# Single source rows by byte addresses on two DMA queues, and a new order at the ends of two graph convolutions

## The chip, the core and the metric

The kernel runs on one core of one Trainium2 chip. The metric is the device time of one execution in microseconds (us), as the median of several runs: 6077.24 us before the change (three runs, 6076.54 to 6078.74). In the profile PE is TensorE (PEld its weight loads), DVE is VectorE, ACT is ScalarE, POOL is GpSimd, and SP is SyncE, which here only issues DMAs. "L767" is line 767 of the kernel before.

## The reference

A graph of N = 6250 nodes with 128 channels and E = 200000 edges, sorted by destination (the destinations are drawn as 6250·u², so low nodes have more edges); `src` is random. After a layer norm and a ReLU come two mesh convolutions and one attention, each over all edges:

```python
def mesh_conv(x, src, dst, ea, w1, b1, g, bt, w2, b2):
    m = jnp.concatenate([x[dst], x[src], ea], axis=-1) @ w1 + b1
    m = jax.nn.silu(group_norm(m, g, bt))
    m = m @ w2 + b2
    out = segment_sum(m, dst); cnt = segment_sum(ones, dst)
    return out / clip(cnt, 1)
h = mesh_conv(x, ...c1);  h = silu(group_norm(h, n1)) + (silu(t_emb) @ tm_w + tm_b)
h = mesh_conv(h, ...c2);  h = silu(group_norm(h, n2)) + x
q, k, v = h @ qw + qb, h @ kw + kb, h @ vw + vb          # 8 heads of 16
logits = (q[dst] * k[src]).sum(-1) * scale + (edge_attr @ ew + eb)
w = softmax of logits over the edges of each dst
o = group_norm(segment_sum(w * v[src], dst) @ ow + ob);  return x + h + o
```

## The kernel before

**Tiles and stages.** Edges lie in order of destination. A tile is 128 edges, a chunk eight tiles (1024 edges), so there are 196 chunks, the last with three tiles. The three stages (`conv(1)`, `conv(2)`, the attention) walk over the same chunks, and each has its own table in DRAM: `b_d` (x @ w1 of the source half, 512 bytes a node) for the convolutions, `kv_d` (keys and values, 1 KB a node) for the attention. The destination half is a product of one-hot matrices with the few table rows (`pk`) that a chunk's destinations span, since these lie close together.

**Fetching the source rows.** `gather` (L767) issues, for each tile, one indirect DMA on GpSimd's queue: 128 rows of the table, chosen by `src`. That is eight per chunk, put into one of the ring's buffers `g` (4 in the convolutions, 11 in the attention). A few chunks are "lone": their eighth tile is not gathered. Class `Rows` (L660) fetches it row by row over many steps: `list_of` loads the 128 node numbers of the tile as one row of a tile (L675), `step` (L678) reads ROWS = 12 of them into registers of SyncE (L689) and issues one DMA per row on SyncE's queue (L693) into the tile `row_g`, and `put` (L700) copies `row_g` into `g` on ScalarE. `by_rows` (L655) chooses the lone chunks: with 12 rows a step a chunk takes 11 steps, so the chunks 16, 27, ... 192, 17 in each stage.

**The steps.** `pipeline` (L878) emits, for each chunk n, one step of the program: `fetch` of chunk n + 2 (its `pk`, the comparison tiles `ohT` for two chunks at a time (L708, L711), and its gathers), then a step of `Rows`, products, roots, the second half of an earlier chunk, and so on; `put` of chunk n + 1 comes late in the step. Each engine runs its instructions in the order of the program (`in_order`). SyncE thus issues the row DMAs between the loads that feed TensorE.

**One chunk in a convolution.** TensorE makes the destination and attribute half (L1227), VectorE adds the gathered half (L1234), ScalarE squares, VectorE sums the squares per group (L1238), ScalarE takes the root (L1245), VectorE inverts and applies three operations (`normed`, L1248 to L1253), ScalarE the silu (L1254), TensorE sums into windows of 128 nodes (`summed`, L1259), ScalarE writes the sum twice under masks (`by_window`, L1264), VectorE adds to the table `U` in SBUF (L1269).

**Node batches.** When no later chunk can reach a window any more, the node part of the layer (`conv_nodes`, L1002: the second weight, group norm, silu, and the products that make the next stage's tables) runs on four windows at once, spread over the steps of the loop: it is a generator, and each step of the loop lets it go on to its next `yield`. `plan_batches` (L376) says at which step a batch starts: in the convolutions every eighth step from 81 to 185, 14 batches; each reads at run time which windows are done, and together they must reach 40 of the 49 windows. What they missed would be mended by a loop that reads its count at run time. `idle=4` makes a batch pause for six steps between its norm and its ends (four in the second convolution), but for the last one. The last nine windows are done after the loop by `last_nodes` (L1157).

**Attention.** `logits` (L1453 to L1459) multiplies the gathered keys with the queries, `maxima` (L1471) does the running maxima of several chunks at once, and per chunk follow the columns (`columns`, ScalarE, L1507, L1655, L1656), the weighted values (L1511), sums, a merge of maxima (L1551, L1525 to L1533) and a late addition. From chunk 170 on (BY_ACT) ScalarE makes the one-hot matrices as well (L1564).

Of the kernel before, what the change touches and what calls it, by code (L numbers as in the profile page):

```python
# [10 lines left out]
I32 = mybir.dt.int32  # L11
AF = mybir.ActivationFunctionType
# [9 lines left out]
P = 128  # L22
D = 128
# [8 lines left out]
BN = 4  # L32
LG = 2
# [4 lines left out]
ROWS = 12  # L38
# [13 lines left out]
def kernel(ctx: ExitStack, tc: tile.TileContext, x, src, dst, eat, w, out):  # L52
# [323 lines left out]
    def plan_batches(i):  # L376
# [278 lines left out]
    def by_rows():  # L655

        span, first = -(-P // ROWS), LG + 3
        return list(range(first + span, NCH - 1, span)), span

    class Rows:  # L660


        def __init__(self, pool, table_d, width):
            self.pool, self.table_d, self.width = pool, table_d, width
            self.chunks, self.span = by_rows()
# [3 lines left out]
            if self.chunks:  # L669
                self.list_of(self.chunks[0])  # L670

        def list_of(self, c):
            t = self.pool.tile([1, P], I32, name="row_at")
            col = c * TPC + TPC - 1
            nc.sync.dma_start(out=t, in_=src[:, col:col + 1].rearrange("p o -> o p"))  # L675
            self.at[c] = t

        def step(self, n):  # L678
            if n in self.starts:
# [6 lines left out]
            if self.now:  # L686
                c, e, t = self.now
                m = min(ROWS, P - e)
                _, at = nc.values_load_multi_w_load_instructions(  # L689
                    self.at[c][0:1, e:e + m], engines=[SP], min_val=0, max_val=N - 1,  # L690
                    skip_runtime_bounds_check_because="a source node")
                for j, a in enumerate(at):
                    nc.sync.dma_start(out=t[e + j:e + j + 1, :], in_=self.table_d[bass.ds(a, 1), :self.width])  # L693
# [184 lines left out]
    def pipeline(i, stage, aside=iter(())):  # L878
# [24 lines left out]
        for n, seconds in enumerate(todo):  # L903
            if n + ahead < NCH:
                ks[n + ahead] = stage.fetch(n + ahead)
            stage.rows.step(n)
# [21 lines left out]
            if n + 1 < NCH:  # L928
                stage.rows.put(ks[n + 1])
# [16 lines left out]
    class Nodes:  # L946
# [14 lines left out]
        def turned(self, t, m, tag="x", silu=None):  # L961
# [3 lines left out]
            if silu:  # L965
                nc.scalar.activation(out, tp, AF.Silu, bias=cols[f"{silu}_b"], scale=cols[f"{silu}_g"])
            else:
                nc.scalar.copy(out, tp)
# [33 lines left out]
    def conv_nodes(b, i, w, m, idle=0, last=False):  # L1002
# [26 lines left out]
        if i == 1 or last:  # L1029
# [5 lines left out]
            tT = b.turned(A, m, "t", silu=f"n{i}")  # L1035
# [21 lines left out]
        for rhs, bias, d_ in ends:  # L1057
            o = b.times(tT, m, rhs)
            if bias:
# [97 lines left out]
    def last_nodes(i, hx=True):  # L1157

        with tc.tile_pool(name="lastn", bufs=1) as lp, tc.tile_pool(name="lastp", bufs=6, space=PSUM) as ps:
# [621 lines left out]
```

## Time and profile before

| | |
|---|---|
| median of three runs | 6077.24 us |
| the profiled execution | 6073.33 us, its span on the core 6071.6 us |
| busy: TensorE | 3607.7 us (59%) |
| busy: VectorE | 4995.9 us (82%) |
| busy: ScalarE | 3351.4 us (55%) |
| busy: GpSimd | 4446.9 us (73%), 4638 gathers |
| mean granted TensorE clock | 0.754 |
| DMA | 760.21 MB, 125 GB/s |

A group of instructions is told with its line, engine, operation and tiles, its count, its busy time, the mean time of one, and behind the bar the idle time of the engine just before these instructions, with what ended that idle time ("issue" is time in which the engine waited for nothing that the profile shows). In a view in order of time each line has its start, its length, its engine and line, and in brackets the idle time before it and who ended it. "SPq" is SyncE's queue of instructions.

### The profile page before, as it was taken

To read this page: it belongs to the slowest core of one execution; us is meant where nothing else is said; L and a number is where in the kernel's file an instruction comes from. 1 tells how busy PE (TensorE), PEld (TensorE's weight loads), DVE (VectorE), ACT (ScalarE), POOL (GpSimd) and SP (SyncE) were. 2 spreads that over 40 slices of the span, in tenths; PEclk is the share of its full clock that TensorE was granted. 3 is DMA by queue.
4 is the path that set the end of the run, shared out by engine and by line. 5 is a ranking of instruction groups with operands and counts; after the bars stand their busy time and mean duration, and the time that the engine had idled before them with its cause. 6 is when DMAs were issued, how large, how long until landed. Compare 5 with 4: busy or idle time off the path is not lost. (4 is left out here: it accounts for less than half of the span.)

```text
span 6071.6 us, 88562 instructions
## 1 busy us (share of the span) xinstructions
PE 3607.7 (59%) x20941; PEld 3418.2 (56%) x20942; DVE 4995.9 (82%) x7118; ACT 3351.4 (55%) x5310; POOL 4446.9 (73%) x4687
## 2 busy tenths in 40 slices
PE   5565556556556555555666666655666665566665
PEld 4555555555556455555555655554555555565554
DVE  7888888888888588878888888865788888888888
ACT  5666666666666566666666666642333333333354
POOL 5777777777777477777777777757777777777775
PEclk8777777777777677777778777776777777777787
DMA  5454343444444343443444444435566666656663
GB/s 159 116 133 120 100 112 101 109 109 104 109 104 111 75 103 97 102 103 100 104 114 115 110 115 111 116 104 155 159 162 165 167 165 166 168 159 168 164 166 85
DMA packets 409874, 760.21 MB, mean 125 GB/s; under 512 B 102703, under 2 KB 276530, under 8 KB 379937
## 3 DMA queue, kind: packets, MB, share of 16 engines
q0 software_dynamic: 173152, 405.57, 26.4%
q1 hardware_dynamic: 230544, 345.24, 21.0%
q10 hardware_dynamic: 5632, 3.50, 0.2%
q8 instruction: 173, 2.83, 0.2%
q14 instruction: 373, 3.06, 0.2%
HBM read 707.36 MB, written 46.58 MB: 124 GB/s over the span
## 5 line engine op out<-in xcount | busy, mean ns | idle before, releaser
L767 POOL DMA_INDIRECT g<-b_d,src_i x3092 | 2931.6, 948 | 954.3 <-issue 904.4
L1259 PE MATMUL u<-h,oh 128*128 128x129 f32 (+1 forms) x6252 | 1265.1, 384 | 1388.4 <-ACT h L1254 1388.2
L1259 PEld LDWEIGHTS u<-h,oh 128*128 128x128 f32 x6252 | 1167.1, 288 | 1469.8 <-ACT h L1254 1465.4
L767 POOL DMA_INDIRECT g<-kv_d,src_i x1546 | 1470.0, 951 | 490.6 <-issue 439.8
L1227 PE MATMUL m<-pk,ohT 101*128 101x128 f32 x6252 | 961.7, 319 | 193.1 <-DVE h L1234 151.7
L1227 PEld LDWEIGHTS m<-pk,ohT 101*128 101x128 f32 x6252 | 932.7, 236 | 210.3 <-DVE h L1234 166.9
L1234 DVE TENSOR_TENSOR h<-m,g 128x1024 f32<-128x1024 f32 x392 | 475.8, 1214 | 477.4 <-DMA g<-b_d,src_i 462.8
L1518 PE MATMUL us<-v,oh 128*128 128x145 f32 x3126 | 590.3, 357 | 378.3 <-DVE flat L1543 329.3
L1518 PEld LDWEIGHTS us<-v,oh 128*128 128x128 f32 x3126 | 545.2, 248 | 418.1 <-DVE flat L1543 241.8
L1438 PE MATMUL qe<-pk,ohT 101*128 101x136 f32 x3126 | 558.1, 348 | 335.0 <-ACT ebs L1455 319.1
L1438 PEld LDWEIGHTS qe<-pk,ohT 101*128 101x128 f32 x3126 | 518.6, 249 | 367.6 <-ACT ebs L1455 360.8
L1254 ACT ACTIVATE h<-h 128x1024 f32<-128x1024 f32 x392 | 412.9, 1053 | 544.5 <-DVE h L1253 527.9
L1236 ACT ACTIVATE sq<-h 128x1024 f32<-128x1024 f32 x392 | 411.8, 1051 | 486.3 <-DVE h L1234 484.1
L733 ACT ACTIVATE ohT<-ohT,minus_p 96x1024 f32<-96x1024 f32 x588 | 669.3, 1138 | 19.6 <-DMA ohT<-rel_d 19.5
L734 ACT ACTIVATE ohT<-ohT 96x1024 f32<-96x1024 f32 x588 | 619.9, 1054 | 18.7
L1238 DVE TENSOR_REDUCE var<-sq 128x64 f32<-128x1024 f32 x392 | 475.0, 1212 | 105.8 <-ACT sq L1236 105.0
L1252 DVE TENSOR_TENSOR h<-h,cps 128x1024 f32<-128x1024 f32 x392 | 477.1, 1217 | 13.5
L1253 DVE TENSOR_TENSOR h<-h,cps 128x1024 f32<-128x1024 f32 x392 | 477.0, 1217 | 13.4
L790 DVE TENSOR_TENSOR oh<-cps,dm 128x1024 f32<-128x1024 f32 x392 | 474.1, 1209 | 2.1 <-PE u L1259 2.1
L1249 DVE TENSOR_TENSOR h<-h,cps 128x1024 f32<-128x1024 f32 x392 | 473.9, 1209 | 0.0
L1453 DVE TENSOR_TENSOR g<-qe,g 128x768 f32<-128x768 f32 (+1 forms) x391 | 251.2, 683 | 211.2 <-DMA g<-kv_d,src_i 203.9
L1531 ACT ACTIVATE us<-d 128x16 f32<-128x16 f32 x196 | 36.6, 187 | 638.2 <-DVE d L1527 566.3
(288 smaller groups left out, 4271.9 us busy)
## 6 DMA issues: line engine op xcount, KB each, us to landing
ohT<-rel_d SPq DMA_DIRECT2D x291, 768.0 KB
row_g<-b_d SPq DMA_DIRECT2D x4352, 0.5 KB
g<-b_d,src_i POOLq DMA_INDIRECT x3092
row_g<-kv_d SPq DMA_DIRECT2D x2176, 1.0 KB
pk<-a_d SPq DMA_DIRECT2D x588, 46.0 KB
g<-kv_d,src_i POOLq DMA_INDIRECT x1546, 3.1
ohT<-in_eat_dram SPq DMA_DIRECT2D x291, 40.0 KB
a_d<-n_o SPq DMA_DIRECT2D x28, 256.0 KB
```

The costliest lines, as they stand in the source:

```text
L733: nc.scalar.activation(k.ohT[:WN, :], k.ohT[:WN, :], AF.Square, bias=minus_p[:WN])
L734: nc.scalar.activation(k.ohT[:WN, :], k.ohT[:WN, :], AF.Relu, bias=1.0, scale=-4.0)
L767: h = nc.gpsimd.indirect_dma_start(out=g[:, t, :table_d.shape[1]], out_offset=None, in_=table_d, in_offset=bass.IndirectOffsetOnAxis(ap=k. ...
L790: return nc.vector.tensor_tensor(k.oh[:, :k.nt, :], iota[:, None, :].to_broadcast([P, k.nt, P]), k.dm[:, :, None].to_broadcast([P, k.nt, P ...
L1227: nc.tensor.matmul(k.m[:, t, :], lhsT=lhs[:, t * P:(t + 1) * P], rhs=rhs, start=(j == 0), stop=(j == len(terms) - 1))
L1234: nc.vector.tensor_tensor(k.mt, k.m[:, :n], k.g[:, :n], ALU.add)
L1238: return lambda: nc.vector.tensor_reduce(var[:, at:at + n * H], sq[:, :n].rearrange("p t (g c) -> p (t g) c", c=HD), AX.X, ALU.add)
L1252: nc.vector.tensor_tensor(k.mt, k.mt, over_edges(gam, k.nt), ALU.mult)
L1253: nc.vector.tensor_tensor(k.mt, k.mt, over_edges(bet, k.nt), ALU.add)
L1259: nc.tensor.matmul(k.u[:, 0, :wide], lhsT=k.oh[:, t, :], rhs=k.h[:, t, :wide], start=(t == 0), stop=(t == k.nt - 1))
L1438: nc.tensor.matmul(k.qe[:, t // TB, at:at + DB], lhsT=lhs[:, t * P:(t + 1) * P], rhs=rhs, start=(j == 0), stop=(j == len(terms) - 1))
L1518: nc.tensor.matmul(k.u[:, :wide], lhsT=k.oh[:, t, :], rhs=k.v[:, t, :wide], start=(t == 0), stop=(t == k.nt - 1))
```

## The change

It has five parts.

1. **Byte addresses and own semaphores.** The list of node numbers is multiplied on VectorE by the bytes of a row (`to_bytes`, four steps after the list was asked for), and the row DMA takes its source from a flat view of the table in bytes, at the register's value. All rows of a step but the last count on a semaphore of the `Rows` object (`landed`), not on those of the framework, and `put` waits for the full count.
2. **More rows.** ROWS goes from 12 to 16: a chunk takes 8 steps, and the lone chunks are 13, 21, ... 189, 23 in each stage. `put` moves to the start of the step.
3. **A second list in the attention.** Another `Rows` object issues nine rows a step on ScalarE's queue, at the end of the step behind the columns: a chunk takes 15 steps, and every 16th chunk from 25 to 185 is lone too, 11 more.
4. **Ends of the convolutions.** The batches start at steps 85 to 181 (13 of them). In the first convolution the last three go without idle steps, and the last two have a step between transpose and silu (`fine` 1), the last one also between each product and its copy (`fine` 2). Chunk 194 is normalised in two halves of four tiles, and before chunk 195 the window copies of 194 are not made first.
5. **The end of the second convolution.** A tile `below` of 12632 floats per partition that nobody uses puts the tiles of `last_nodes(2)` higher in SBUF.

```diff
-ROWS = 12
+ROWS = 16
+BY_SIDE = 9
+BELOW = 12632
...
-            if n % 8 == (4 if i == 3 else 1) and n > (40 if i == 3 else 80) and n + 6 < NCH \
+            if n % 8 == (4 if i == 3 else 5) and n > (40 if i == 3 else 80) and n + (6 if i == 3 else 10) < NCH \
...
-    def by_rows():
-        span, first = -(-P // ROWS), LG + 3
-        return list(range(first + span, NCH - 1, span)), span
+    def by_rows(m, every, first=LG + 3):
+        span = -(-P // m)
+        return list(range(first + span, NCH - 1, every)), span
...
+            self.bytes_d = table_d.rearrange("n c -> (n c)").bitcast(U8)
+            self.landed = [[tc.alloc_semaphore(f"{name}{j}"), 0] for j in range(2)]
...
+        def to_bytes(self, t):
+            nc.vector.tensor_scalar(t, t, 4 * self.width, None, ALU.mult)
         def step(self, n):
+            self.fresh -= 1
+            if self.fresh == 0:
+                self.to_bytes(self.at[max(self.at)])
...
                 for j, a in enumerate(at):
-                    nc.sync.dma_start(out=t[e + j:e + j + 1, :], in_=self.table_d[bass.ds(a, 1), :self.width])
+                    h = self.issue.dma_start(out=t[e + j:e + j + 1, :].bitcast(U8),
+                                             in_=self.bytes_d[bass.ds(a, 4 * self.width)][None, :])
+                    if j == m - 1:
+                        tc.declare_fence(h.ins, group=key)
+                        continue
+                    tc.no_tile_sem_insts.add(h.ins.name)
+                    h.then_inc(s[0], 16)
+                    s[1] += 16
...
         def put(self, k):
             if k.c in self.got:
-                nc.scalar.copy(k.g[:, TPC - 1, :self.width], self.got.pop(k.c))
+                s = self.landed[self.chunks.index(k.c) % 2]
+                nc.scalar.copy(k.g[:, TPC - 1, :self.width], self.got.pop(k.c)).wait_op(s[0], s[1], "sem-ge")
...
-            stage.rows.step(n)
+            if n + 1 < NCH and n + 1 in ks:
+                for r in stage.rows:
+                    r.put(ks[n + 1])
+            stage.rows[0].step(n)
...
             if n < NCH:
                 stage.early(ks, n, todo[n + 1])
-            if n + 1 < NCH:
-                stage.rows.put(ks[n + 1])
+            for r in stage.rows[1:]:
+                r.step(n)
...
-            tT = b.turned(A, m, "t", silu=f"n{i}")
+            tp = b.in_bank(A, m)
+            if fine > 0:
+                yield
+            tT = b.silu_of(tp, m, f"n{i}")
...
             o = b.times(tT, m, rhs)
-            if bias:
+            if bias or fine > 1:
                 yield
...
+            if i == 2:
+                es.enter_context(tc.tile_pool(name="below", bufs=1)).tile([P, BELOW], FP, name="below")
...
-            def normed(k):
+            def normed(k, by=TPC):
+                for a in range(0, k.nt, by):
+                    n = min(by, k.nt - a)
+                    mt = k.mt[:, a:a + n]
...
-                        if k.c >= NCH - SOON and self.sums:
+                        if NCH - SOON <= k.c < NCH - 1 and self.sums:
...
-                        normed(k)
+                        normed(k, TPC // 2 if k.c == NCH - 2 else TPC)
...
-                    for r in conv_nodes(nodes, i, w, BN, idle=4 if j + 1 < len(plans[i]) else 0):
+                    for r in conv_nodes(nodes, i, w, BN, idle=4 if j + (3 if i == 1 else 1) < len(plans[i]) else 0,
+                                        fine=(j + 3 - len(plans[i])) * (i == 1)):
...
-                self.rows = Rows(rw, kv_d, KV)
+                self.rows = [Rows(rw, kv_d, KV, "rows3"),
+                             Rows(side, kv_d, KV, "rows4", mybir.EngineType.Activation, BY_SIDE, 16, 10)]
```

More of the change, by code (lines that the diff above doesn't have):

```diff
@@ L653, with __init__ @@
         oh = pe = v = None
-    def by_rows():
-        span, first = -(-P // ROWS), LG + 3
-        return list(range(first + span, NCH - 1, span)), span
+    def by_rows(m, every, first=LG + 3):
+        span = -(-P // m)
+        return list(range(first + span, NCH - 1, every)), span
     class Rows:
-        def __init__(self, pool, table_d, width):
-            self.pool, self.table_d, self.width = pool, table_d, width
-            self.chunks, self.span = by_rows()
+        def __init__(self, pool, table_d, width, name, engine=SP, m=ROWS, every=-(-P // ROWS), first=LG + 3):
+            self.engine, self.m, self.issue = engine, m, nc.sync if engine == SP else nc.scalar
+            self.pool, self.table_d, self.width, self.name = pool, table_d, width, name
+            self.bytes_d = table_d.rearrange("n c -> (n c)").bitcast(U8)
+            self.chunks, self.span = by_rows(m, every, first)
+            self.landed = [[tc.alloc_semaphore(f"{name}{j}"), 0] for j in range(2)]
             self.starts = {c - 2 - self.span: c for c in self.chunks}
@@ L670, in __init__ @@
                 self.list_of(self.chunks[0])
+                self.to_bytes(self.at[self.chunks[0]])
+                self.fresh = 0
         def list_of(self, c):
-            t = self.pool.tile([1, P], I32, name="row_at")
+            t = self.pool.tile([1, P], I32, name="row_at", bufs=2)
             col = c * TPC + TPC - 1
@@ L687, in step @@
                 c, e, t = self.now
-                m = min(ROWS, P - e)
+                m = min(self.m, P - e)
                 _, at = nc.values_load_multi_w_load_instructions(
-                    self.at[c][0:1, e:e + m], engines=[SP], min_val=0, max_val=N - 1,
-                    skip_runtime_bounds_check_because="a source node")
+                    self.at[c][0:1, e:e + m], engines=[self.engine], min_val=0, max_val=(N - 1) * 4 * self.width,
+                    skip_runtime_bounds_check_because="where a source node's row begins")
+                s = self.landed[self.chunks.index(c) % 2]
+                key = f"{self.name}_{c}_{e}"
                 for j, a in enumerate(at):
-                    nc.sync.dma_start(out=t[e + j:e + j + 1, :], in_=self.table_d[bass.ds(a, 1), :self.width])
+                    h = self.issue.dma_start(out=t[e + j:e + j + 1, :].bitcast(U8),
[6 more added lines that the diff above has]
+                    s[1] += 16
+                    tc.add_to_no_dep_group(key, h.ins)
                 self.now[1] = e + m
@@ L959, in in_bank, with turned, silu_of @@
             return tp[:, :m, :]
-        def turned(self, t, m, tag="x", silu=None):
+        def turned(self, t, m, tag="x"):
             tp = self.in_bank(t, m)
             out = self.tile(m, tag)
[L965 to L968, printed above, removed]
+            nc.scalar.copy(out, tp)
+            return out
+        def silu_of(self, tp, m, n):
+            out = self.tile(m, "t")
+            nc.scalar.activation(out, tp, AF.Silu, bias=cols[f"{n}_b"], scale=cols[f"{n}_g"])
             return out
@@ L1000, in span, with conv_nodes @@
         return bass.ds(w, m) if not isinstance(w, int) else slice(w, w + m)
-    def conv_nodes(b, i, w, m, idle=0, last=False):
+    def conv_nodes(b, i, w, m, idle=0, last=False, fine=0):
         at = span(w, m)
@@ L1157, in last_nodes @@
     def last_nodes(i, hx=True):
[L1159 removed]
+        with ExitStack() as es:
+            if i == 2:
+                es.enter_context(tc.tile_pool(name="below", bufs=1)).tile([P, BELOW], FP, name="below")
+            lp = es.enter_context(tc.tile_pool(name="lastn", bufs=1))
+            ps = es.enter_context(tc.tile_pool(name="lastp", bufs=6, space=PSUM))
             n = NW - NWD
@@ L1278, in fetch @@
                     k.g = gp.tile([P, TPC, D], FP, name="g")
-                    gather(k, k.g, b_d[i], ring, self.rows.chunks)
+                    gather(k, k.g, b_d[i], ring, self.rows[0].chunks)
                     k.h = hs[c % len(hs)]
@@ L1356, in conv @@
             stage = Stage()
-            stage.rows = Rows(rw, b_d[i], D)
+            stage.rows = [Rows(rw, b_d[i], D, f"rows{i}")]
             nodes.var = lambda: stage.var[:, NV:]
@@ L1586, in fetch @@
                 k.g = gp.tile([P, TPC, KV], FP, name="g")
-                self.behind = gather(k, k.g, kv_d, ring, self.rows.chunks)
+                self.behind = gather(k, k.g, kv_d, ring, self.rows[0].chunks + self.rows[1].chunks)
                 return k
```

16 lines of the change are left out of this document (10 added, 6 removed).

## The prediction

> **What bounds it.** I read the page first, then GpSimd (POOL) in order of time, then the waits of SyncE's queue, then the two places between stages, then ScalarE in the attention.
>
> ```profile
> span 6071.6 us, 88562 instructions
> ...
> L767 POOL DMA_INDIRECT g<-b_d,src_i x3092 | 2931.6, 948 | 954.3 <-issue 904.4
> ...
> L767 POOL DMA_INDIRECT g<-kv_d,src_i x1546 | 1470.0, 951 | 490.6 <-issue 439.8
> ```
>
> GpSimd issues 4638 gathers of 0.95 us; nearly all its idle time before them is "issue", about 0.3 us each, so it waits for nobody. The table by stretches, cut where the rows of gathers begin and end (columns: length, then busy time and count of PE, PEld, DVE, ACT and POOL, granted clock, share of the DMA engines, GB/s):
>
> ```profile
> 56.00:1995.00 1939.00, 1144.99 (x6728) 1095.99 (x6726) 1609.67 (x1787) 1261.25 (x1555) 1467.04 (x1546) 0.75 0.44 112
> 2060.00:3995.00 1935.00, 1156.35 (x6747) 1104.44 (x6748) 1618.01 (x1660) 1251.04 (x1533) 1463.95 (x1546) 0.75 0.42 108
> 4049.00:5990.00 1941.00, 1184.46 (x6748) 1104.76 (x6748) 1593.07 (x3305) 739.94 (x2017) 1469.11 (x1546) 0.76 0.61 164
> 1995.00:2060.00 65.00, 34.40 (x172) 32.24 (x172) 35.90 (x66) 34.70 (x54) 5.95 (x3) 0.63 0.09 24
> 3995.00:4049.00 54.00, 29.75 (x176) 27.19 (x174) 32.59 (x60) 20.10 (x33) 6.04 (x2) 0.75 0.23 63
> 5991.00:6071.00 80.00, 33.65 (x191) 30.91 (x191) 63.76 (x151) 16.73 (x61) 24.84 (x35) 0.69 0.08 22
> ```
>
> Each stage is one unbroken row of 1546 gathers, so one costs 1939/1546 = 1.254 us, then 1.252 and 1.256. The three rows make 5815 us of the span. The rest is 56 us of preparation, two gaps of 65 and 54 us, and 80 us after the last gather. A change pays if it takes gathers out of the rows or shortens a gap.
>
> **The gathers.** Before, every 11th chunk from 16 to 192 has its eighth tile fetched by single rows: 17 chunks. After, SyncE does every 8th from 13 to 189, 23 chunks, and in the attention ScalarE's queue does every 16th from 25 to 185, 11 more, none of them twice. That takes 6, 6 and 17 gathers out: 7.5, 7.5 and 21.4 us. Near the end of the attention this stops paying, as the waits of VectorE there show, first for 4100 to 5600 us, then for 5730 to 6050 us:
>
> ```profile
> DVE g L1453 <- DMA g<-kv_d,src_i: 165.1, 49, 11.6
> ```
> ```profile
> DVE g L1453 <- DMA g<-kv_d,src_i: 7.9, 3, 5.1
> ```
> ```profile
> 5832.17 0.95 DVE L1453 TENSOR_TENSOR g<-qe,g 128x768 f32<-128x768 f32 x1
> ```
>
> VectorE lives on the gathers until chunk 178, whose first product this last row is, the last to start within 4 us of its gathers; then it has a backlog of its own. One gather of the 17 lies net behind chunk 178 (two by SyncE and one by ScalarE, where before there were two), so I count 16: 20.1 us. Sum: 35.1 us.
>
> **The price on SyncE.** It issues the rows between the loads that feed TensorE. Here are the instructions of a row (shortest/median/longest, ns), the load of a step's addresses, and one step of twelve rows:
>
> ```profile
> L693 SPq FUSED_REGOPS  x6528: 37/37/47, 95.0 to 5956.6; - x198
> ...
> L693 SPq DMA_DIRECT2D row_g<-b_d x4352: 224/228/1167, 95.1 to 3941.2; - x198
> ```
> ```profile
> L689 SPq TENSOR_LOAD <-row_at x561: 687/1007/2876, 93.9 to 5947.2; - x187
> ```
> ```profile
> 654.41 4.79 SPq L693 DMA_DIRECT2D row_g<-b_d  x12
> ```
>
> And SyncE's longest waits, from 400 to 1600 us in the first convolution and from 4400 to 5600 us in the attention (121 steps each; us in total, times, longest):
>
> ```profile
> SPq L708 <- PE m L1227: 130.0, 38, 7.1
> SPq L693 <- DMA ohT<-rel_d: 99.6, 61, 3.4
> ```
> ```profile
> SPq L693 <- DMA ohT<-rel_d: 136.3, 60, 5.4
> SPq L708 <- PE qe L1438: 136.0, 31, 9.5
> ```
>
> A row takes (4.79 − 0.23)/11 = 0.41 us when nothing holds it. With byte addresses the multiplication by the row's length should go: 0.037 us and about as much behind it, so 0.34 is my value, 0.41 the upper bound. Twelve rows and a load (1.01) were 5.95 us; sixteen are 6.6 us at 0.34, or 7.8 at 0.41, with 0.17 more for the load of sixteen addresses. So SyncE gets 0.65 to 1.8 us more per step. Its waits give 1.90 us a step in the convolution and 2.25 in the attention; the larger half of the landing waits goes too, since fifteen of sixteen rows now count on a semaphore of their own. It fits: no cost. If that cover is gone, SyncE is late with pk and ohT and everything stands behind it (the slower rival).
>
> [...]
>
> New on VectorE is one multiplication of a 1x128 list per lone chunk, 80 in all. The nearest row is a small one:
>
> ```profile
> 2040.21 0.17 DVE L1008 TENSOR_SCALAR n_c<-flat 128x3 f32<-128x3 f32 x1 [2.33 <-DMA wcl<-wc_d]
> ```
>
> 14 us, spread over stretches in which VectorE waits for gathers: nothing, and 0.2 us after chunk 178. It comes four steps after its list is asked for and four before SyncE reads it, so neither waits. The copy into place now stands at the head of ScalarE's step and waits for the rows; behind it are the root and the comparisons. The last rows are issued two steps, some 20 us, earlier: nothing.
>
> **The price on ScalarE.** Nine rows come after each step's columns. Here is ScalarE in the attention, from the end of the columns to what comes next:
>
> ```profile
> 5259.06 0.20 ACT L1656 CAST v<-ef 128x8 f32<-128x8 bf16 x1
> 5263.10 0.19 ACT L1531 ACTIVATE us<-d 128x16 f32<-128x16 f32 x1 [3.83 <-DVE d L1527]
> 5263.22 0.20 ACT L1533 ACTIVATE be<-d 128x16 f32<-128x16 f32 x1
> 5264.62 0.27 ACT L1455 COPY ebs<-qe 128x48 f32<-128x48 f32 x2 [1.20 <-DVE g L1453]
> ```
>
> The hole is 3.8 us, and 1.2 more before the next operation that VectorE asks for soon. Nine rows at 0.34 to 0.41 and a load of about 0.9 are 4.0 to 4.6 us: hidden within 5.0. In steps 179 to 182 ScalarE also makes the one-hot matrices (from chunk 170 on), and VectorE has no slack left there; I put 3 us on that; the bounds are 0 and 8 (2 us late in each of the four, see the rival). [...]
>
> **The first convolution's end.** The last gather ends at 1995 us, and the last chunk's use of it comes 26 us later; in the second convolution (3995 us) it is 7.6 us:
>
> ```profile
> 2021.11 0.55 DVE L1234 TENSOR_TENSOR h<-m,g 128x384 f32<-128x384 f32 x1
> ```
> ```profile
> 2005.95 0.58 ACT L1067 COPY n_o<-nd 128x512 f32<-128x512 f32 x1 [5.18 <-PE nd L974]
> ```
> ```profile
> 4002.60 0.55 DVE L1234 TENSOR_TENSOR h<-m,g 128x384 f32<-128x384 f32 x1
> ```
>
> ScalarE stands 5.18 us before the copy of a node batch, whose product was given to TensorE just ahead of it, while the next silu waits behind. The change starts the last batch at step 181 instead of 185, lets the last three go without idle steps, and puts a step between product and copy (and between transpose and silu). Its steps end at 193. I take a lag of 10 us in place of 26, nearer to the second convolution's, since one wait of this kind a step is what sets the two apart: 16 us; the bounds are 0 and 18.4. There are 13 batches instead of 14. They still reach the 40 windows: the last one counts on chunk 177, whose first edge goes to node 5127 in the list that the reference draws, and window 40 begins at 5120.
>
> **The end of both convolutions.** Chunk 194 is normalised in halves, and chunk 195 no longer stands behind the window copies of 194:
>
> ```profile
> 2028.85 1.06 ACT L1254 ACTIVATE h<-h 128x1024 f32<-128x1024 f32 x1 [2.82 <-DVE h L1253]
> 2033.80 0.72 ACT L1264 ACTIVATE u<-u,mask 128x129 f32<-128x129 f32 x2 [3.90 <-PE u L1259]
> ...
> 2036.70 0.72 ACT L1264 ACTIVATE u<-u,mask 128x129 f32<-128x129 f32 x2 [1.75 <-PE u L1259]
> ```
> ```profile
> 4018.34 0.68 DVE L1065 TENSOR_TENSOR n_o<-nd,r_qb 128x512 f32<-128x512 f32 x1
> ```
> ```profile
> 4036.95 4.94 SPq L1062 DMA_DIRECT2D kv_d<-n_o  x6
> ...
> 4044.01 1.80 SPq L1074 DMA_DIRECT2D h_d<-n_x  x3
> ```
> ```profile
> 4049.09 0.95 POOL L767 DMA_INDIRECT g<-kv_d,src_i  x1 [18.81 <-DMA ohT<-in_eat_dram]
> ```
>
> TensorE sums eight tiles in the 3.9 us from 2029.9 to 2033.8. With halves the first silu waits for three operations on half the width, some 0.65 us each by the 0.55 of the 384 wide row above, not for three at double that; it can start 1.9 us earlier and takes half as long, so TensorE begins near 2027.5 and ends near 2031.5; chunk 195's three tiles follow at once, to 2033.0 instead of 2036.7. I take 3.6 us, and 3.4 in the second convolution, whose order is the same; the bounds are 0 and 4. In the second convolution the last batch's query end (4018.34 to 4019.02) stands behind the loop, and SyncE still has to issue its write before the branch. Started four steps earlier, it ends at step 194: I take 2.0 us for the two and their signal, between 0.7 and 2.0, and 1.5 less lag. Last, the node tiles of the end lie 50 KB higher, above the attention's gather buffers. So the first gather no longer waits for the h_d writes (issued until 4045.81, first gather 3.3 us later), only for the kv_d writes (issued until 4041.89): 3.9 us, bounds 0 and 3.9.
>
> **Sum.** 35.1 + 16 + 3.6 + 3.4 + 2.0 + 1.5 + 3.9 − 3 = 62.5 us. The profiled execution took 6073.33 us (span 6071.6), 3.9 under the median of the three runs, so it stands for them: 6077.2 − 62.5 = 6014.7, given as 6015.
>
> **Rivals.** *The gathers alone* (chance 0.20): the lag at 1995 us comes from other things than the copies, and the first attention gather waits for something else in those buffers. Then 19.9 us go: 6035. For it speaks that VectorE's own work there is dense; against it, the 5.18 us wait.
>
> *SyncE sets the pace, slower* (0.06): at 0.41 us a row its spare 1.90 us is used up. From 0.417 on, each step is longer than the gathers'. At 0.43 (a row that waits a little) it is 0.21 us × 184 steps × 3 stages, 116 us, with the gathers' gain gone and some 27 us kept at the ends: 6165. For it: SyncE waits in most steps for an earlier landing. Against it: most rows leave that chain.
>
> *ScalarE late in the attention* (0.06): a row costs 0.54 us, as on SyncE with waits, so load and rows take 5.8 us in a hole of 3.8 to 5.0 and ScalarE is 0.8 to 2.0 us late. VectorE's spare is 165.1 us over 151 steps, 1.1 us each; from there on it decides. At 2.0 us, 0.9 us are lost in each of 165 steps, 149 us, the gathers' 20 with them: 6184. At the lower end little is lost: near 6035.
>
> *The transfers bind* (0.03): the share of the DMA engines in the attention is 0.61 (table above), and the same bytes move. Were that the limit, the attention's 20.1 us would stay: 6035. The gathers' 0.3 us "issue" before each speaks against it. [...]
>
> **How the numbers follow.** The forecast has 0.63, a rest of 0.02 is open. The range goes from 5998 (lag as in the second convolution or less, ScalarE at no cost, shorter steps) to 6045 (the gathers alone, with 8 us on ScalarE). Faster by over 0.2% (12 us, about what a measurement of this kernel can tell): forecast, gathers alone, transfers, half of ScalarE's case and the rest, 0.88; within 0.2%: 0.04; slower: 0.08.
>
> **What would show it.** After: 1540, 1540 and 1529 gathers at 1.25 us with "issue" before them; a row of SyncE near 0.34 us and no multiplication; the first gap near 45 us, the second near 43; ScalarE's nd waits (L1067) small after 1980 us; VectorE's waits for gathers in the attention still over 100 us. The forecast is wrong if gathers show waits for ring buffers, if SyncE's waits on TensorE vanish, or if the first gap stays near 65 us.

## The result, and the profile after

The changed kernel takes 6031.62 us (median of four runs, 6023.66 to 6035.83), the kernel before 6077.99 (four runs, 6076.54 to 6081.23): a ratio of 0.992, with a 95% interval of 0.990 to 0.994, or 46 us less. The forecast was 6015, 62.5 us less; 16 us of the sum are missing. The profiled execution of the changed kernel took 6035.83 us, the slowest of its four, with a span of 6033.9, against 6073.33 (3 us under the fastest of the four) and 6071.6 before. What follows compares these two executions first; their spans lie 38 us apart, not 46, so 25 us of the sum are missing between them.

The page of the changed kernel, span and gathers:

```profile
span 6033.9 us, 89776 instructions
...
L793 POOL DMA_INDIRECT g<-b_d,src_i x3080 | 2925.2, 950 | 953.8 <-issue 903.8
...
L793 POOL DMA_INDIRECT g<-kv_d,src_i x1529 | 1457.3, 953 | 482.7 <-issue 433.9
```

The counts are the forecast ones, 1540 a convolution and 1529 in the attention, and nearly all idle time ahead of them is still "issue": GpSimd waits for nobody. The table by stretches, cut as before where the rows of gathers begin and end (length, then PE, PEld, DVE, ACT, POOL busy, clock, DMA share, GB/s):

```profile
56.00:1991.00 1935.00, 1139.06 (x6758) 1090.93 (x6756) 1622.79 (x1811) 1276.68 (x1576) 1463.06 (x1540) 0.75 0.44 112
2034.70:3966.00 1931.30, 1143.54 (x6734) 1091.77 (x6734) 1617.94 (x1672) 1251.45 (x1537) 1462.05 (x1540) 0.74 0.42 108
4011.00:5937.00 1926.00, 1210.60 (x6654) 1132.06 (x6655) 1585.01 (x3304) 725.57 (x1989) 1457.28 (x1529) 0.75 0.62 165
1991.00:2034.70 43.70, 23.07 (x110) 21.58 (x110) 23.64 (x56) 20.24 (x34) 5.74 (x3) 0.66 0.09 25
3966.00:4011.00 45.00, 25.47 (x146) 23.52 (x146) 28.71 (x56) 18.75 (x32) 5.76 (x1) 0.73 0.15 42
5937.00:6034.00 97.00, 48.25 (x287) 44.35 (x286) 79.14 (x189) 34.58 (x108) 24.83 (x35) 0.76 0.09 25
```

Held against the table of before, the three rows of gathers are 4, 4 and 15 us shorter (the forecast had 7.5, 7.5 and 21.4), the gaps 21 and 9 us (forecast 19.6 and 10.8), and the tail after the last gather is 17 us longer: 97 us in place of 80 (16 us when both are taken from the end of the last gather, 97.0 and 80.7). So two things are off: the rows give about 13 us too little, and the tail takes 17 us where the forecast had some 4 (3 us for ScalarE's list and 1.3 us for the gather behind chunk 178).

**SyncE** did what the forecast said. One step of sixteen rows, and the two instructions of a row (shortest/median/longest, ns):

```profile
663.62 5.14 SPq L710 DMA_DIRECT2D row_g<-b_d  x16
```
```profile
L710 SPq MOVE row_g<-b_d x5888: 29/29/38, 95.6 to 3881.3; - x197
L710 SPq DMA_DIRECT2D row_g<-b_d x5888: 224/228/1266, 95.7 to 3881.3; - x197
```

The multiplication is gone, and a row takes (5.14 − 0.23)/15 = 0.33 us, where 0.34 was put.

**The first convolution's end.** The last chunk's addition, and VectorE's first node operation after the loop:

```profile
1996.02 0.55 DVE L1272 TENSOR_TENSOR h<-m,g 128x384 f32<-128x384 f32 x1
...
2013.89 0.17 DVE L1039 TENSOR_SCALAR n_c<-flat 128x3 f32<-128x3 f32 x1 [4.82 <-issue]
```

The addition comes 5 us after the last gather's end, not 26: 21 us gained, more than the 18.4 that the forecast set as the bound. ScalarE's waits for node products, 11.7 us from 1960 us on before, are gone from the same stretch. Behind it the halves save what they were to save: from the addition to the first node operation it takes 17.9 us, where it took 19.1, although VectorE stands 4.82 us ahead of that operation, where it stood 2.33 before; without these 2.5 us it is 3.7 us less, and the forecast had 3.6. "Issue" says that the profile has no releaser for the wait. The trace shows where it lies: VectorE's branch at the loop's end begins at 2009.46, its next instruction only at 2012.51, 3.0 us later, where before these two lie 0.6 us apart (2038.27 and 2038.83). Why, it does not show.

**The attention.** VectorE's longest waits from 4062 to 5560 us, then from 5690 to 6010:

```profile
DVE g L1496 <- DMA g<-kv_d,src_i: 108.4, 41, 10.1
DVE v L1554 <- ACT v L1550: 60.1, 34, 6.2
```
```profile
DVE flat L1580 <- ACT us L1574: 24.6, 5, 8.3
DVE lg L1502 <- ACT ebs L1498: 7.2, 3, 4.6
DVE v L1554 <- ACT v L1550: 6.5, 10, 2.2
```

The same waits before, from 4100 to 5600 and from 5730 to 6050 us:

```profile
DVE v L1511 <- ACT v L1507: 6.7, 18, 0.4
```
```profile
DVE flat L1537 <- ACT us L1531: 15.2, 4, 5.3
DVE v L1511 <- ACT v L1507: 3.2, 8, 0.5
DVE lg L1459 <- ACT ebs L1455: 2.0, 1, 2.0
```

In the first stretch nearly all of the 60 us of waits for ScalarE's copies are new, and the waits for gathers fall by about as much, from 165 to 108: VectorE's spare pays. In the second, the wait for the factors us (L1574) rises from 15.2 to 24.6 us and its longest from 5.3 to 8.3; with the two other waits for ScalarE it is 17.9 us more. Here is the step in which it happens, on ScalarE and on VectorE:

```profile
5795.26 1.06 ACT L1608 ACTIVATE oh<-oh 128x1024 f32<-128x1024 f32 x1
5797.55 3.05 ACTq L710 DMA_DIRECT2D row_g<-kv_d  x9
5800.64 0.19 ACT L1574 ACTIVATE us<-d 128x16 f32<-128x16 f32 x1 [4.33 <-issue]
```
```profile
5800.86 0.44 DVE L1580 TENSOR_TENSOR flat<-flat,us 128x272 f32 x1 [6.83 <-ACT us L1574]
...
5820.57 0.44 DVE L1580 TENSOR_TENSOR flat<-flat,us 128x272 f32 x1 [8.35 <-ACT us L1574]
```

The one-hot matrix ends at 5796.3; then come a load of addresses and nine rows, and only then the factors for which VectorE has been waiting since 5794.0. The chunks' first products, 2 to 13 us behind their gathers until chunk 178 in both executions, are 24.6 us behind at chunk 182 (11.3 before) and 46.5 at the last (29.3 before). That is the 17 us of the tail.

### The profile page after: what moved, and what is told of

Its sections match the earlier page's. It is cut to its first block, busy times and chain, and to the rows that moved or that the text cites. A ratio compares the mean times of both kernels' runs of the same rounds, so it can differ in the third digit from the quotient of the medians.

```text
span 6033.9 us, 89776 instructions
## 1 busy us (share of the span) xinstructions
PE 3613.9 (60%) x20869; PEld 3426.5 (57%) x20870; DVE 4999.1 (83%) x7176; ACT 3353.8 (56%) x5332; POOL 4427.8 (73%) x4658
## 5 line engine op out<-in xcount | busy, mean ns | idle before, releaser
L1265 PE MATMUL m<-pk,ohT 101*128 101x128 f32 x6252 | 942.6, 315 | 168.6 <-DVE h L1272 121.8
L1265 PEld LDWEIGHTS m<-pk,ohT 101*128 101x128 f32 x6252 | 913.4, 232 | 185.8 <-DVE h L1272 137.5
L1481 PE MATMUL qe<-pk,ohT 101*128 101x136 f32 x3126 | 586.0, 361 | 328.3 <-ACT ebs L1498 280.5
L1561 PEld LDWEIGHTS us<-v,oh 128*128 128x128 f32 x3126 | 557.7, 253 | 380.3 <-DVE flat L1586 200.0
L1481 PEld LDWEIGHTS qe<-pk,ohT 101*128 101x128 f32 x3126 | 543.8, 260 | 361.3 <-ACT ebs L1498 332.7
L1296 ACT ACTIVATE h<-h 128x1024 f32<-128x1024 f32 (+2 forms) x394 | 413.4, 1049 | 577.1 <-DVE h L1295 563.1
L1294 DVE TENSOR_TENSOR h<-h,cps 128x1024 f32<-128x1024 f32 (+2 forms) x394 | 477.5, 1212 | 13.5
L1295 DVE TENSOR_TENSOR h<-h,cps 128x1024 f32<-128x1024 f32 (+2 forms) x394 | 477.4, 1212 | 13.5
L1291 DVE TENSOR_TENSOR h<-h,cps 128x1024 f32<-128x1024 f32 (+2 forms) x394 | 474.1, 1203 | 0.0
L1574 ACT ACTIVATE us<-d 128x16 f32<-128x16 f32 x196 | 36.5, 186 | 494.2 <-DVE d L1570 331.6
```

Source lines behind the costliest of these rows:

```text
L1265: nc.tensor.matmul(k.m[:, t, :], lhsT=lhs[:, t * P:(t + 1) * P], rhs=rhs, start=(j == 0), stop=(j == len(terms) - 1))
L1294: nc.vector.tensor_tensor(mt, mt, over_edges(gam, n), ALU.mult)
L1295: nc.vector.tensor_tensor(mt, mt, over_edges(bet, n), ALU.add)
L1481: nc.tensor.matmul(k.qe[:, t // TB, at:at + DB], lhsT=lhs[:, t * P:(t + 1) * P], rhs=rhs, start=(j == 0), stop=(j == len(terms) - 1))
L1561: nc.tensor.matmul(k.u[:, :wide], lhsT=k.oh[:, t, :], rhs=k.v[:, t, :wide], start=(t == 0), stop=(t == k.nt - 1))
```

## The experiments

Theory: the tail is lost because ScalarE's last list (chunk 185, rows in steps 168 to 182) runs into the steps in which ScalarE makes the one-hot matrices. Rival: VectorE's own backlog sets the end, so gathers that end earlier only make the tail longer. The first four runs and the last three (nineteen rows as ten and nine, and the two after it) were on two chips on which the kernel before itself takes 8476 and 8485 us; there the times say little about a kernel that is bound by its gathers (see the last section). They are told for what they show beside it.

**The changed kernel again, and three versions, on the first of those chips.** No edit:

> The changed kernel once more, beside the three below, since its four times spread over 12 us (6023.7 to 6035.8) and its profiled execution was the slowest. Theory: the spread belongs to the kernel and comes from single gathers that take over 1.3 us (36 us of excess in the profiled execution, 24 us before the change), so the median here lies between 6024 and 6036 and the excess is again above that of before. Rival: the extra long gathers were chance; then the excess is near 24 us and the time near 6020.

Measured: 8414.6 us against 8475.6 before, ratio 0.992 (0.990 to 0.995); of the long gathers nothing can be read, since gathers there wait for other engines (27.02 us ahead of the one at 5012.68 us).

The list of ScalarE ended early:

```
-    Rows(side, kv_d, KV, "rows4", mybir.EngineType.Activation, BY_SIDE, 16, 10)]
+    Rows(side, kv_d, KV, "rows4", mybir.EngineType.Activation, BY_SIDE, 16, 10, 180)]
```

(the last number is the bound of its chunks; 169 is then the last one)

> ScalarE's list in the attention ends with chunk 169 instead of 185, so no row of it is issued while ScalarE also makes the one-hot matrices (chunks 170 and up). One gather more. Theory (ScalarE is late in those steps: VectorE waited 6.8 and 8.3 us for its factors there, and never gets it back): the tail after the last gather falls from 96 to about 80 us, the time is about 6031.6 - 15 = 6017. Rival (the tail is long because the gathers end earlier and VectorE's own backlog decides the end): the tail stays near 95, and the time is 6032 to 6033.

Measured: 8402.2 us, ratio 0.991 (0.988 to 0.995). The tail is 109 us, as in the run before it (111): inconclusive.

No list on ScalarE:

```
-    self.rows = [Rows(rw, kv_d, KV, "rows3"),
-                 Rows(side, kv_d, KV, "rows4", mybir.EngineType.Activation, BY_SIDE, 16, 10)]
+    self.rows = [Rows(rw, kv_d, KV, "rows3")]
```

> No list on ScalarE at all: 1540 gathers in the attention instead of 1529, everything else of the change kept. Theory (ScalarE's lateness at the end eats what its list saves): 11 x 1.26 = 13.9 us more in the row of gathers, about 15 less in the tail: 6030, within 4 us of the changed kernel. Rival (ScalarE's list costs nothing, the tail has another cause): 6045.

Measured: 8397.4 us, ratio 0.990 (0.986 to 0.993): inconclusive.

The kernel before with the ends alone (the new plan of batches, `fine`, the halves, chunk 195's order, the tiles that lie higher; the old `Rows`):

> The kernel before with only the two edits to the ends of the convolutions and the tiles that lie higher; rows on SyncE as before (twelve, by node numbers), none on ScalarE. Theory: the gaps fall as in the changed kernel, 65 to 43 and 54 to 44 us, the gathers' rows and the tail stay: 6078 - 32 = 6046, and the excess of long gathers stays near 24 us. Rival (part of the shorter gaps comes from SyncE, whose rows no longer wait for landings): the first gap stays above 48 us and the time above 6051.

Measured: 8424.1 us, ratio 0.992 (0.989 to 0.995): inconclusive. The four ratios overlap.

**The list ended early, on another chip** (before: 6081.5 us), the same edit:

> ScalarE's list ends with chunk 169, once more: the chip of the first four runs held SyncE up (8475 us for the kernel before), so that the tail said nothing there. On a chip that runs the kernel before in about 6078 us. Theory (ScalarE late in the steps with one-hot matrices): tail about 80 us in place of 97, time about 6017, a ratio of 0.990. Rival (VectorE's own backlog): tail near 95 us, time 6032 to 6033, a ratio of 0.9925.

Measured: 6020.28 us (6018.63 to 6027.21), ratio 0.990 (0.988 to 0.992). The attention's row, the tail, and VectorE's waits from 5690 us on:

```profile
4007.10:5936.20 1929.10, 1197.37 (x6735) 1120.87 (x6736) 1599.88 (x3340) 742.12 (x2028) 1462.18 (x1530) 0.76 0.62 165
...
5936.20:6018.40 82.20, 39.29 (x207) 36.04 (x205) 62.47 (x152) 19.33 (x68) 24.76 (x35) 0.68 0.07 22
```
```profile
DVE flat L1580 <- ACT us L1574: 15.2, 4, 5.2
```

The gathers end at the same time as in the changed kernel (5936), with one gather more, and the tail is 82 us instead of 97; the wait for us is back at the 15.2 us of before. The rival, which wanted 95, falls. The intervals of the two ratios, 0.988 to 0.992 here and 0.990 to 0.994 for the changed kernel, overlap, so the tail decides and not the times. This is the best version of the study: 61 us under the kernel before. That it comes so near to the forecast's 62.5 is luck in part: by the profiles its rows of gathers give 20 us where the forecast had 35, and its two gaps 34 where it had 30.

**No list on ScalarE**, on a third chip (before: 6086.2 us), the edit as above:

> The change without any list on ScalarE (1540 gathers in the attention). Theory (what ScalarE's list saves in the row it loses at the end): row 11 x 1.26 = 13.9 us longer, tail about 82 in place of 97: 6030. Rival (the list costs nothing): 6045.

Measured: 6035.16 us (6031.96 to 6036.9), ratio 0.9915 (0.990 to 0.993), where the changed kernel has 0.992 on its chip: the same.

```profile
4009.90:5949.80 1939.90, 1171.31 (x6732) 1092.23 (x6733) 1596.73 (x3329) 744.53 (x2021) 1469.71 (x1540) 0.77 0.62 165
1993.00:2034.00 41.00, 22.25 (x107) 20.62 (x105) 20.29 (x53) 18.39 (x33) 5.67 (x3) 0.67 0.10 27
...
5949.80:6033.00 83.20, 35.41 (x210) 32.30 (x208) 64.73 (x153) 19.67 (x70) 24.58 (x35) 0.72 0.07 21
```

The row of gathers is 13.9 us longer than the changed kernel's (1939.9 against 1926.0), the tail 13.8 us shorter (83.2 against 97.0). About 5 us of the longer row belong to the chip, where the median interval of two gathers is 1.252 us (1.249 on that of the changed kernel). VectorE's waits for ScalarE's copies are at 6.7 us again, so it is this list that made them 60. So the whole list on ScalarE, eleven gathers, brings nothing that these runs can tell as long as its last chunk stays in.

**The ends alone**, on the same chip as the last:

> The kernel before with only the edits to the ends of the convolutions and the tiles that lie higher. Theory: the gaps fall as in the changed kernel, 64.6 to 43 and 53.8 to 43, the rows and the tail stay: 6080 - 32 = 6048, long gathers near 24 us of excess. Rival (part of the shorter gaps comes from SyncE's rows): first gap above 48, time above 6053.

Measured: 6048.23 us (6047.68 to 6054.67), ratio 0.994 (0.993 to 0.9955), 38 us under before.

```profile
1998.30:2035.40 37.10, 20.49 (x108) 19.31 (x107) 20.15 (x53) 18.15 (x33) 5.64 (x2) 0.69 0.11 31
3974.30:4017.50 43.20, 25.65 (x146) 23.68 (x146) 27.57 (x55) 18.47 (x31) 5.84 (x3) 0.73 0.14 41
5967.70:6046.50 78.80, 37.15 (x175) 32.99 (x175) 58.30 (x150) 16.33 (x60) 24.61 (x35) 0.67 0.07 22
```

The first gap is even shorter than in the changed kernel (37 against 44); the rival falls, and the sign is the other way: with parts 1 and 2 of the change the first gap is some 4 us longer (41.0 with them, 37.1 without, on the same chip) and the tail 4.4 (83.2 against 78.8). Of the 4 us in the gap, 2.5 are VectorE's wait behind its branch: 4.82, 4.94 and 4.91 us in the changed kernel and the two runs above, 2.33 in this run and before. It is not the rows that make it: the next run has sixteen of them, without byte addresses, and waits 2.33 us. The tail of one execution differs by about 2 us from that of another with the same rows (80.7 before, 78.8 here). SyncE's eighteen gathers are the difference of these two runs: 13 us, of which the rows of gathers give 20.

**Sixteen rows a step without the bytes.** The kernel before with

```
-ROWS = 12
+ROWS = 16
```

> The kernel before with sixteen rows a step in place of twelve, by node numbers, each row with the semaphore of its own kind as before (0.41 us a row and the waits for landings). 18 gathers less. Theory (bytes and the shared semaphore make the room on SyncE): four rows more are 1.64 us plus a third more of the landing waits, against 1.07 us of waits for TensorE in the convolutions; SyncE is late by about 0.8 us a step, 184 steps x 2 stages, 300 us less 22 of gathers: about 6350, at least slower than before. Rival (SyncE has room anyway): 18 x 1.25 = 22 us faster, 6058.

Measured: 6403.5 us, ratio 1.053 (1.051 to 1.054): slower, as the theory had it. Of SyncE's waits for TensorE from 400 to 1600 us 3.4 us are left; thirteen rows in a stretch take 6.45 us, and the gathers' idle time grows by 292 us over both groups:

```profile
649.68 6.45 SPq L693 DMA_DIRECT2D row_g<-b_d  x13
```
```profile
L767 POOL DMA_INDIRECT g<-b_d,src_i x3080 | 2935.0, 953 | 1084.6 <-issue 895.9
...
L767 POOL DMA_INDIRECT g<-kv_d,src_i x1540 | 1462.9, 950 | 652.0 <-issue 450.3
```

A step is 10.43 us in the first convolution (115 steps in 1200 us, where there were 121). The prediction's slower rival is real. What keeps the change out of it is its first part (byte addresses and a shared semaphore) with the copy moved to the start of the step; these were not tried one without the other.

**Nineteen rows a step**, on top of the version that ends at 169:

```
-ROWS = 16
-BY_SIDE = 9
+ROWS = 19
+BY_SIDE = 10
...
-    Rows(side, kv_d, KV, "rows4", mybir.EngineType.Activation, BY_SIDE, 16, 10, 180)]
+    Rows(side, kv_d, KV, "rows4", mybir.EngineType.Activation, BY_SIDE, 14, 12, 180)]
```

> The version of the run before (ScalarE's list ends ahead of the one-hot matrices), now with nineteen rows a step on SyncE (27 chunks a stage in place of 23) and ten rows a step on ScalarE (12 chunks up to 179 in place of 10). Gathers: 1536, 1536, 1524. Theory (gathers set the pace, SyncE's spare is 1.5 us a step, ScalarE's hole takes one row more): 14 gathers of 1.25 us less, 17.5 us: about 6003 where the version with sixteen takes 6020. Rival (SyncE's spare is used up: three more rows are 0.97 us a step, and the loads come late): the mean interval of the gathers rises above 1.27 us, 6030 to 6100.

Measured: 6634.75 us, ratio 1.090 (1.088 to 1.091); the theory falls, and by more than its rival. Nineteen rows take 6.06 us, as 0.33 each would have it, but the load of their addresses takes over three times what sixteen took (4.10 us in the median, against 1.23). The loads on SyncE (L704; count, then shortest/median/longest in ns), first of the changed kernel, then of this one over the whole run, and from 676 to 690 and at 713 us:

```profile
L704 SPq TENSOR_LOAD <-row_at x552: 1131/1234/3577, 94.3 to 5878.0; - x184
L704 ACTq TENSOR_LOAD <-row_at x165: 657/2143/2962, 4106.1 to 5851.6; - x165
```
```profile
L704 SPq TENSOR_LOAD <-row_at x567: 1784/4097/6489, 92.3 to 6543.0; - x189
```
```profile
L704 SPq TENSOR_LOAD <-row_at x2: 4078/4112/4146, 678.4 to 689.9; - x2
```
```profile
L704 SPq TENSOR_LOAD <-row_at x1: 1863/1863/1863, 712.8 to 712.8; - x1
```

The long ones begin at entries 19 and 38 of the list, the short one at entry 76. Taken over all 81 lists: loads that begin at entries 0 and 76 have medians of 2.04 and 1.86 us, those at 19, 38, 57 and 95 have 4.13. In this run, then, the loads that begin at a multiple of four entries (16 bytes) are the short ones, and the others take about double. The same holds for ScalarE's nine in the changed kernel: entries 0, 36, 72 and 108 take 0.96 us, the others 2.14 to 2.64, except the two addresses at the end (0.66). Here are loads from entries 9 to 27, then the one from entry 36:

```profile
L704 ACTq TENSOR_LOAD <-row_at x3: 2147/2151/2169, 4589.3 to 4613.1; - x3
```
```profile
L704 ACTq TENSOR_LOAD <-row_at x1: 956/956/956, 4621.9 to 4621.9; - x1
```

Twelve and sixteen addresses always begin at such a multiple.

**Nineteen rows in the convolutions, loaded as ten and nine**, with the attention of the version that ends at 169:

```
+                half = m if m <= 16 else 10
...
-                for j, a in enumerate(at):
+                for j in range(m):
+                    if j % half == 0:
+                        at = load(j, min(half, m - j))
+                    a = at[j % half]
...
-            stage.rows = [Rows(rw, b_d[i], D, f"rows{i}")]
+            stage.rows = [Rows(rw, b_d[i], D, f"rows{i}", m=19, every=7)]
```

> The version whose list on ScalarE ends with chunk 169, and in the two convolutions nineteen rows a step on SyncE, their addresses loaded as ten, ten rows, nine, nine rows; the attention as in that version. 8 gathers less. The nineteen rows of the run before this took one load of 3.46 us a step, where sixteen addresses took 1.31 and twelve 1.07, and no wait was left on SyncE. Theory (that load is what made it slow): loads of ten and nine are about 0.95 and 0.9 us, SyncE's step 11.0 - 3.46 + 1.85 = 9.4 us against the gathers' 9.8, so the gathers keep the pace: 8 x 1.25 = 10 us less than 6020, 6010. Rival A (nineteen rows of 0.33 us are too many by themselves): a step stays above 10.5 us and the time above 6300. Rival B (SyncE's spare is used up, the loads come late in some steps): 6020 to 6100, gathers waiting for VectorE's additions.

Measured, on the second of the two chips that hold SyncE up: 9172.4 us against 8484.7, ratio 1.081 (1.077 to 1.084). The theory's price was wrong, by the beginnings just told: most of these loads begin off a multiple of four, and in the convolutions their median is 2.12 us, not 0.9. Ten addresses from entry 76 take 1.18 us in the median, ten from 19, 38, 57 or 95 take 2.32; nine from 48 take 1.02, nine elsewhere 2.07 to 2.12. Whether nineteen rows with loads that begin right would pay stays open; it wasn't tried.

**The tiles of the second convolution's end where they were:**

```
-    es.enter_context(tc.tile_pool(name="below", bufs=1)).tile([P, BELOW], FP, name="below")
```

> The version whose list on ScalarE ends with chunk 169, with the node tiles of the second convolution's end where they lay before (under the attention's gather buffers). Theory (the first attention gather then waits for the writes out of those tiles): the second gap is 41.9 + 3.9 = 46 us, the time 6024. Rival (it waits for something as late anyway): the gap stays within 1 us of 42.

Measured on the same chip: 8412.4 us; second gap 67.2 us, against 67.6 in the version that keeps them (on the other held-up chip). The gap as a whole shows nothing, since what stands ahead of the last writes differs by more from run to run. The order at its end shows the theory. First this run, then the next one, which keeps the tiles high, on the same chip:

```profile
5354.39 4.17 SPq L1096 DMA_DIRECT2D kv_d<-n_o  x6
...
5360.68 1.83 SPq L1108 DMA_DIRECT2D h_d<-n_x  x3
...
5365.85 0.95 POOL L793 DMA_INDIRECT g<-kv_d,src_i  x1 [17.65 <-DMA pk<-a_d]
```
```profile
5337.79 4.17 SPq L1096 DMA_DIRECT2D kv_d<-n_o  x6
...
5344.08 1.60 SPq L1108 DMA_DIRECT2D h_d<-n_x  x3
...
5344.69 0.95 POOL L793 DMA_INDIRECT g<-kv_d,src_i  x1 [13.10 <-ACT n_x L994]
```

With the tiles where they were, the first gather comes 3.3 us after the last h_d write and 7.3 after the last kv_d write was issued (3.3 and 7.2 in the kernel before). With the tiles high it comes while h_d is still being written, 2.7 us after the last kv_d write (2.7 to 3.2 in the changed kernel and four other runs). So the first gather does wait for the h_d writes without the tile `below`, and the tile is worth 4.0 to 4.6 us, where 3.9 was put; the rival falls.

**The node batches as before** (`n % 8 == 1`, `n + 6 < NCH`, idle steps for all but the last batch, no `fine`):

> The version whose list on ScalarE ends with chunk 169, with the node batches of the convolutions as before: 14 in place of 13, the last started at step 185 and with idle steps, product and copy in one step. Halves of chunk 194 and the order of chunk 195 kept. Theory (the batches beside the last chunks made the lag): first gap 42 + 16 = 58 us, second 42 + 3.5 = 45.5, time 6020 + 19.5 = 6040. Rival (the order of the last chunks made most of it): first gap below 50, time below 6030.

Measured on the same chip: 8421.7 us, ratio 0.993 (0.991 to 0.9955). The first gap, and for comparison that of the run before, which has the new plan (the tile `below` is of the second convolution alone):

```profile
2653.20:2730.60 77.40, 40.26 (x212) 38.02 (x212) 43.44 (x76) 44.50 (x67) 5.60 (x1) 0.68 0.09 24
```
```profile
2657.70:2719.80 62.10, 35.23 (x178) 33.00 (x177) 41.50 (x73) 36.17 (x55) 5.63 (x3) 0.67 0.08 23
```

15 us in a gap of 62, where the theory had 16 in one of 42. The batches made the lag; the rival falls. Of the 3.5 us expected in the second gap 0.8 can be seen: from the last gather to the end of the kv_d writes it takes 60.7 us here and 59.9 with the new plan.

## Why the prediction was right, and where its sum was off

**The bound** was right: GpSimd's gathers pace all three stages, before and after, and the rows got shorter by taking gathers out of them.

**SyncE at no cost**: nearly right. Rows of 0.33 us fit, and the case where they don't was shown (0.41 with a landing wait each: 5.3% slower). Not foreseen was that with parts 1 and 2 the first gap and the tail are longer, by some 8 us together in one pair of profiles, so that eighteen gathers bring 13 us instead of 22.5. Why the ends get longer was not settled; 2.5 us of it are VectorE's wait behind its branch, and some 2 us of the tail are within what executions differ by.

**The gathers' 35.1 us**: the price per gather held (median interval 1.249 us before and after), but the changed kernel's profiled execution has more long ones. Summed over the intervals above 1.3 us, the excess over 1.249 is 23.5 us before and 35.3 after, and this is most of the 13 us by which the rows fall short; with twelve rows (ends alone) it is 26.8, with sixteen in two other runs 28.3 and 29.9. Part of it may go with the rows, 2 to 6 us by these runs; the rest varies with the execution: this one was the slowest of its four. What makes a gather long stays open.

**The first convolution's lag, 16 us**: the mechanism was right, as the plan of batches put back shows (15 us there); with the other edits the lag fell by 21. **The ends together**: 30.4 us were forecast, 38 measured by the run with the ends alone. That the changed kernel's own gaps fell by just 30 is luck in part: the lag gave 5 us more than was put, VectorE's wait behind its branch took 2.5 of them back, and the second gap gave 2 less. **`below`, 3.9 us**: right, by the order of the writes and the first gather; of the 3.5 us of the second convolution's batches the run with the old plan shows 0.8.

**The step that failed** is the "3 us" for ScalarE in steps 179 to 182, and with it the reading of its hole. The list costs 14 us there (97.0 − 83.2), and 15 by the run that ends it at chunk 169 (97.0 − 82.2), outside the bounds of 0 and 8. No run shows the 3 or the bound of 0; what the runs show is the 14 and the 15. Two parts of that step were wrong. First, the load of nine addresses was put at 0.9 us; ten of fifteen take over 2.1 us. With nine rows (3.05) that is 5.2 us in a hole of 5.0, and the new 60 us of waits for v are the sign of it; there the wait for gathers hid them. Second, in the steps with one-hot matrices I took each to be 2 us late at most. But the rows stand behind the one-hot matrix and ahead of the factors, and VectorE waited 6.8 and 8.3 us. Nor did the load and the rows run under the comparisons, as the trace shows. The load of that step, from 5790 to 5800 us:

```profile
L704 ACTq TENSOR_LOAD <-row_at x1: 2153/2153/2153, 5795.3 to 5795.3; - x1
```

It begins with the last operation of the one-hot matrix (5795.26), which waits by a semaphore for the eight comparisons before it (the eighth ends at 5795.22), and not earlier; the rows begin 1.2 us after that operation's end. All 165 loads of this list begin within 0.4 us of the start of the operation just ahead of them.

The version that ends the list at chunk 169 shows that this term is what went wrong in the tail: all other terms kept but one gather, the tail is at 82 us and the time 61.2 us less than before. It does not show that the rest of the sum was right: there, too, the rows give less and the gaps more than was put.

**Rivals.** *The gathers alone*: no. By its time alone the result, 6031.6, is nearer to this rival's 6035 than to 6015; the gaps tell the two apart, since they fell by 30 us, as forecast, and the rows and the tail fell short. *Transfers bind*: no, the attention's row is shorter by 15 us with seventeen gathers less at nearly the same bytes (758.7 MB over the whole kernel, 760.2 before). *ScalarE late in the attention*: it was, but under cover, until step 179. *SyncE sets the pace*: not at 0.33 us a row; at 0.41 and with the waits for landings, yes.

## What to carry to other kernels

When work is moved to a queue that is idle on average, look at the steps in which that engine has extra work, and end the moved work before them: here one chunk of eleven cost about what all eleven brought. Where an engine's spare is small against the price of a new piece, price every instruction of the piece by a row of the same form; a load of nine addresses was not a load of twelve scaled down. And a wait that an engine shows is not all room: SyncE's 1.5 us a step did not carry three more rows whose load had grown.

## What the runs showed of the hardware that was not expected

**In these runs the time of a load of addresses into registers went with where it began.** Beginning at a multiple of 16 bytes: 0.56 us for four (SyncE's 147 loads at L649), 1.01 for twelve, 1.23 for sixteen, 0.96 for nine, 1.17 for ten. Beginning elsewhere: 2.15 for nine, 2.36 for ten, 4.13 for nineteen (1.86 to 2.04 when it begins right); the two addresses at the end of ScalarE's list, from entry 126, took 0.66. It was seen on SyncE and ScalarE and on three chips (those of the changed kernel, of the nineteen rows, and of the ten and nine). This is what five lists and that of the run with ten and nine show; no run changed the beginning alone. VectorE takes 0.34 us for its loads at L649 (median of 147), where SyncE takes 0.56.

**Two queues were tied together.** With ScalarE's list, SyncE's load of its next list waits in the attention (4400 to 5600 us) for a row:

```profile
SPq L683 <- DMA row_g<-kv_d: 126.7, 15, 9.5
```

Without it, this wait is gone, and SyncE waits for TensorE instead (202.8 us in 42 waits). The trace's semaphores show the tie: the last row of a step, on either queue, counts on one of the same eight semaphores as SyncE's loads, in turn, and waits there for the last user. No gather was seen to wait for it.

**On two chips SyncE is held up by something else.** There the kernel before takes 8476 and 8485 us. Sixteen rows in a step, and the register move ahead of a row, in the changed kernel there:

```profile
5023.44 14.40 SPq L710 DMA_DIRECT2D row_g<-b_d  x16
```
```profile
L710 SPq MOVE row_g<-b_d x5888: 1/29/1457, 121.9 to 5192.3; - x197
```

The move ahead of a row takes 29 ns on the other chips (38 at most). Here SyncE's moves take close to 700 ns in 1127 of 9562 cases, ScalarE's in 108 of 1413, and the starts of neighbouring instructions on SyncE lie 0.68 to 0.72 us apart 2608 times (13 times in the first profile of the same kernel). The gather at 5012.68 us came after a wait of 27.02 us, where nearly all gathers of the first profile stand 0.3 us behind the one before, and the load of pk for TensorE behind the sixteen rows is issued at 5038.03. At 1.25 us each the 4609 gathers are 5761 us of a span of 8385.6; there they are no longer the bound. The trace does not show the cause.
